# Finding the edges of 16 graphs on VectorE, and showing by sums that a matrix holds only zeros and ones

## The chip, the cores and the metric

The kernel runs on one core of a Trainium2 chip. The metric is the device time of one run in microseconds; lower is better. Five engines work side by side: TensorE (PE, with its weight loads as PEld), VectorE (DVE), ScalarE (ACT), GpSimd (POOL) and SyncE (SP, which here only issues transfers).

## The reference, cut to what matters

There are 16 graphs of 1024 nodes with 64 features each. `adj` is a symmetric float32 matrix of zeros and ones, drawn at random, 1024 x 1024 for each graph. Layer 0 thins the neighbours of each node, takes three weighted quantiles of their features and runs a small MLP; layer 1 is three graph convolutions.

```python
h = jnp.maximum(_layernorm(x), 0.0)
# layer 0
adj_ = jnp.where(eye, 1.0, adj);  neigh = (adj_ > 0) & ~eye
rank = jnp.cumsum(ni, axis=-1) - ni;  nb = ni.sum(-1)         # ni = neigh as int
skip = jnp.where(nb > 10, (nb + 1) // 2, 1)
rem = neigh & (skip > 1) & (rank % skip == skip - 1) & mask   # then rem | rem^T
nd = where(rem, 0, adj_) > 0                                  # the live neighbours
s = jnp.sort(where(nd[..., None], h[:, None], inf), axis=2)   # quantiles 0.25, 0.5, 0.75
x = x + (relu((h + agg) @ W1 + b1) @ W2 + b2) * mask
# layer 1
h = jnp.maximum(_layernorm(x), 0.0)
x1 = bn(relu(adj @ (h @ W1) + b1)); x2 = ...; x3 = ...        # adj as it is, not only its sign
x = x + relu(concat(x1, x2, x3) @ Wl + bl)
```

What matters for the change is that layer 0 only asks whether an entry is above zero, while layer 1 multiplies with the entries themselves. A kernel that stores the matrix as one byte of 0 or 1 per entry is right for both only if every entry is exactly 0 or 1. Both kernels therefore carry a flag that says whether any entry was something else; if it is raised, a second, general path computes everything again. With the inputs here the flag stays down.

## The kernel before

**Pairs.** The graphs go in eight pairs. `prepare(p, pools)` makes all that layer 0 needs of pair p; it is written as a generator, and each `yield` in it ends a step. The main part first runs `prepare(0)` to its end, with nothing beside it. Then, for each pair, it goes through seven blocks of nodes (`gather_block`, `sort_block`), and before each block it takes 11 steps of the next pair's `prepare`. So pairs 1 to 7 are prepared under the gathering and sorting of the pair before. After the last pair's preparation come its own blocks, woven with the second phase (`later`: the MLP and layer 1), and then the flag.

**Order.** A scheduler fixes the order of the instructions on each engine when the kernel is built; it follows the order of the program loosely, and an engine then takes its instructions strictly in that order. Buffers of one tag in a pool are used in rotation, in the order of the program: a tag with `bufs=1` has one buffer, so that the next user of the tag must wait until the one before it is done. Within a pool all calls share the tags, so graph x=0 and graph x=1 of a pair do.

**Preparing one graph** (`prepare_one`, L651 to L844). The matrix goes through in eight tiles of 128 rows:

- a transfer on SP's queue loads the tile `a`, 512 KB of float32, into one of two buffers (L661);
- ACT takes the sign of it into `edge`, one byte an entry (L662);
- DVE computes (a == 1) != a with one instruction, which is 1 where an entry is neither 0 nor 1, and sums it along each row into `odd` (L664); the entries themselves go to a scrap tile `junk_v`;
- PE transposes the tile of `edge` by eight matmuls with the identity into `ptE` in PSUM (L669), in one of two buffers of the tag "big";
- ACT copies `ptE` to `edgeT` (L672).

After the eight tiles `edgeT` is written to DRAM for layer 1 (L676), and the neighbours are counted and ranked: sums over chunks (L648), a few small DVE instructions, eight matmul groups with ACT (`stays`, L717) and DVE (L718), eight with ACT again (L744, which overwrites `edge` with the live neighbours and sums them into `nv`). The nodes are then ranked by the number of live neighbours: eight ACT passes (L762), each of which compares `keys` with one node per row and writes its entries to a scrap tile of the tag "junk" (one buffer), while the sums go to `above`. DVE turns those into `place` (L765), and POOL sends the rows of `edge` to their places in DRAM (L770).

When both graphs are that far, `find_live` reads the rows back and transposes them to `liveT` (L786 to L799), and checks by sums that the degrees lie where the blocks expect them: `by` compares sums with a table `bounds` (L817), and L820 sums what is beyond, with its entries going to the tag "junk" too. `number_slots` numbers the neighbours of each node into `r` (L838). `prepare` ends with `z` (L611 to L614) and the features in three bfloat16 parts, `hp` (L620 to L624).

**Gathering.** For each block and group of slots DVE compares `r` with the slot's number into `s` (L962, two buffers), PE multiplies `s` with `hp` into `pg` (L993), and ACT copies it to `g` (L998). `sort_block` sorts `g` on DVE (L920 and others).

**Bounds and flag.** The table `bounds` is made at setup, L470 to L490: POOL fills lines of 1024 and sends them to rows of `bounds` by transfers, 16 lines with two transfers each. The flag, L1409 to L1424, takes the largest of `odd` in each row and the largest of `beyond`, brings the rows together with one transpose on PE, and compares with 0.

Of the kernel before, what the change touches and what calls it, by code (L numbers as in the profile page):

```python
# [9 lines left out]
F32 = mybir.dt.float32  # L10
F16 = mybir.dt.float16
BF16 = mybir.dt.bfloat16
F8 = mybir.dt.float8e4
# [3 lines left out]
ALU = mybir.AluOpType  # L17
# [4 lines left out]
P = 128  # L22
# [377 lines left out]
def graph_layers_kernel(ctx: ExitStack, tc: tile.TileContext, ins, out: bass.AP):  # L400
# [61 lines left out]
    bounds = const.tile([C, HALF], BF16, name="bounds")  # L462
# [7 lines left out]
    with tc.tile_pool(name="setup", bufs=2) as setup:  # L470
        for c in range(1, NT + 1):
            most, least = [(-float(N), 0, N)], [(0.0, 0, N)]
            for (j0, j1, few, slots), (first, end, fewer) in zip(BLOCKS + (TAIL,), NEAR):
                if c == NT:
                    least.append((float(few), j0, j1))
                    most.append((-float(slots), j0, j1))
                    for k in sorted(fewer, reverse=True):
                        most.append((-float(k), j0, j0 + fewer[k]))
                if c in first:
                    most.append((-float(first[c]), j0, j1))  # L480
                if c in end:
                    least.append((float(end[c]), j0, j1))
            for row, pieces in ((c - 1, most), (NT + c - 1, least)):
                line = setup.tile([1, N], BF16, tag="line", name="line")
                for value, a, b in pieces:
                    nc.gpsimd.memset(line[:, a:b], value)
                for hf in range(NH):
                    nc.gpsimd.dma_start(
                        out=bounds[32 * hf + row : 32 * hf + row + 1, :], in_=line[:, hf * HALF : (hf + 1) * HALF]
                    )  # L490

    odd = const.tile([P, NB, NT], F32, name="odd")
# [74 lines left out]

    h_d = [dram.tile([N, C], F32, name=f"h_d{b}") for b in range(NB)]
# [14 lines left out]
    def prepare(p, pools):  # L583

        work, keep, ps = pools
        st = Pair()
        st.p = p
# [63 lines left out]
    def prepare_one(st, x, pools):  # L651
# [7 lines left out]
        for t in range(NT):  # L659
            a = work.tile([P, N], F32, tag="a", bufs=2, name="a")  # L660
            nc.sync.dma_start(out=a, in_=adj_d[b, t * P : (t + 1) * P, :])  # L661
            nc.scalar.activation(edge[:, t, :], a, AF.Sign, saturate=False)  # L662
            junk = work.tile([P, N], F8, tag="junk_v", name="junk_v")
            nc.vector.scalar_tensor_tensor(  # L664
                junk, a, 1.0, a, ALU.is_equal, ALU.not_equal, accum_out=odd[:, b, t : t + 1], saturate=False
            )
            pt = ps.tile([P, NT, P], F32, tag="big", bufs=2, name="ptE")
            for u in range(NT):
                nc.tensor.matmul(  # L669
                    out=pt[:, u, :], lhsT=edge[:, t, u * P : (u + 1) * P], rhs=ident_h, start=True, stop=True  # L670
                )
            nc.scalar.activation(edgeT[:, :, t * P : (t + 1) * P], pt, AF.Copy, saturate=False)  # L672
            if t % 2:
                yield
# [105 lines left out]
        def find_live():  # L780
# [31 lines left out]
            for hf in range(NH):  # L812
# [4 lines left out]
                    out=by[:, sl], lhsT=ident_h[rows, rows], rhs=bounds[rows, :], start=False, stop=True  # L817
# [531 lines left out]
    with ExitStack() as stack:  # L1349
# [7 lines left out]
        with ExitStack() as inner:  # L1357
# [3 lines left out]
            )  # L1361

# [46 lines left out]
    with ExitStack() as stack:  # L1409
        ps = stack.enter_context(tc.tile_pool(name="ps_flag", bufs=1, space=PSUM))  # L1410
        most_odd = const.tile([P, 1], F32, name="most_odd")
        nc.vector.tensor_reduce(most_odd, odd.rearrange("p b t -> p (b t)"), AX.X, ALU.max)
        worst = const.tile([P, 1], F32, name="worst")
        nc.vector.tensor_copy(worst, most_odd)
# [6 lines left out]
        nc.vector.tensor_reduce(most, pd, AX.X, ALU.max)  # L1421
        nc.vector.tensor_scalar(most, most, 0.0, None, ALU.is_gt)
# [30 lines left out]
```

## Time and profile before

| | us |
|---|---|
| three runs of the kernel | 3240.37, 3244.12, 3251.95 (median 3244.12) |
| the profiled execution | 3232.01 |
| its span in the profile | 3230.2 |
| DVE busy | 2569.1 (80%) |
| PE busy | 2602.9 (81%) |
| ACT busy | 1714.2 (53%) |
| POOL busy | 461.8 (14%) |
| L664, DVE check of a tile | 156.3 in 128 instructions of 1.221 |
| L669, PE transposes of a tile | 1024 matmuls |
| L762, ACT ranking passes | 144.4 in 128 instructions of 1.128 |
| L962, DVE compares for gathering | 621.1 in 1312 instructions |
| L993, PE gathering matmuls | 1361.8 in 16848 instructions |
| load of `a`, issue to landing | 3.4 |

The profile is of one execution, and its span is 1.8 us shorter than that execution's own time. An engine's share is its busy time over the span, an average over stretches that have different limits. The mean granted TensorE clock in this execution is 0.902 of the full one. In the tables of groups, the words after the line and the engine are the operation, what it writes <- what it reads, and the shapes; then come the busy time in us, the mean of one in ns, and the idle time of that engine just before these instructions with what ended most of it. In a timeline each row is a start in us from the span's start, a length, the engine, the line and the operation, and in square brackets a wait that ended just before with what ended it.

### The profile page before, as it was taken

How to read it: one execution, taken by the hardware profiler on the slowest of the kernel's cores; microseconds unless marked ns; L12 is line 12 of the kernel's file. 1: busy time of each engine (PE TensorE's matmuls, PEld its weight loads, DVE VectorE, ACT ScalarE, POOL GpSimd, SP SyncE). 2: the span in 40 equal slices, each digit the busy share in tenths (PEclk: the TensorE clock that was granted, in tenths of full speed). 3: DMA queues.
4: the chain of work that ended last, by engine and by line, in shares of the span. 5: the costliest groups of instructions: out<-in, count | busy, mean ns of one | idle time of the engine just before them, and what ended most of it. 6: DMA issues, size and time to landing. Idle time of an engine off the chain costs nothing. (4 is left out here: it accounts for less than half of the span.)

```text
span 3230.2 us, 67236 instructions
## 1 busy us (share of the span) xinstructions
PE 2602.9 (81%) x27819; PEld 1728.7 (54%) x27849; DVE 2569.1 (80%) x5895; ACT 1714.2 (53%) x3292; POOL 461.8 (14%) x545
## 2 busy tenths in 40 slices
PE   3689968987898689867686799689976689898878
PEld 2446645664566357545463466456644356565545
DVE  4149999899889988998997889988996888793332
ACT  4777647655766566666464666476553223242221
POOL 4111020110011001200112010201112120221110
PEclk9779989998999799988797799889988799899999
DMA  4131113011311130114001211130102110222211
GB/s 136 46 105 66 37 44 123 33 35 32 118 33 37 42 107 33 51 54 97 31 17 45 91 48 34 45 117 32 39 21 61 21 42 17 54 55 53 53 53 41
DMA packets 221082, 177.45 MB, mean 55 GB/s; under 512 B 189024, under 2 KB 189152, under 8 KB 216672
## 3 DMA queue, kind: packets, MB, share of 16 engines
q1 hardware_dynamic: 141824, 125.88, 12.7%
q0 software_dynamic: 17408, 37.81, 3.8%
q10 hardware_dynamic: 61536, 9.39, 1.9%
q8 instruction: 219, 3.59, 0.5%
q14 instruction: 95, 0.78, 0.1%
HBM read 124.44 MB, written 48.55 MB: 54 GB/s over the span
## 5 line engine op out<-in xcount | busy, mean ns | idle before, releaser
L993 PE MATMUL pg<-s,hp 128*64 128x400 bf16 (+11 forms) x16848 | 1361.8, 314 | 93.2 <-DVE s L962 92.7
L993 PEld LDWEIGHTS <-hp 128*64 128x64 bf16 x16848 | 907.4, 113 | 452.1 <-issue 75.3
L962 DVE TENSOR_SCALAR s<-r 128x3200 bf16<-128x3200 bf16 (+25 forms) x1312 | 621.1, 520 | 144.2 <-PE pg L993 143.9
L998 ACT COPY g<-pg 128x400 f32<-128x400 f32 (+10 forms) x384 | 168.5, 442 | 478.2 <-PE pg L993 440.4
L920 DVE TENSOR_TENSOR t<-g 128x600 f32<-128x600 f32 (+9 forms) x524 | 319.8, 628 | 12.9 <-ACT g L998 11.1
L770 POOL DMA_INDIRECT live_d<-edge,place x128 | 175.4, 1371 | 1025.3 <-DVE place L765 870.9
L1129 PE MATMUL pg<-adjT,xw 128*64 128x512 fp8e4 x2304 | 285.5, 400 | 39.6 <-DVE xw L1119 28.9
L920 DVE TENSOR_TENSOR g<-t 128x96 f32<-128x96 f32 (+16 forms) x555 | 285.8, 539 | 1.4
L855 ACT ACTIVATE coef<-z,bias 128x200 f32<-128x200 f32 (+6 forms) x480 | 174.8, 402 | 140.9 <-DVE agg L933 133.7
L1129 PEld LDWEIGHTS <-xw 128*64 128x64 bf16 x2304 | 144.7, 115 | 163.1 <-DVE xw L1119 30.3
L1172 POOL DMA_INDIRECT agg<-agg_d,place x128 | 139.4, 1089 | 535.7 <-PE pt L1060 412.8
L920 DVE TENSOR_TENSOR t<-t 128x192 f32<-128x192 f32 (+20 forms) x447 | 208.5, 478 | 0.4
L796 PE MATMUL pt<-ident_h,lp 128*128 128x128 bf16 x1024 | 102.3, 261 | 120.8 <-DMA lp<-live_d 71.1
L786 POOL DMA_DIRECT2D lp<-live_d x128 | 87.5, 685 | 774.0 <-PE pt L796 745.4
L664 DVE SCALAR_TENSOR_TENSOR junk_v<-a 128x1024 fp8e4<-128x1024 f32 x128 | 156.3, 1221 | 49.2 <-DMA a<-in_adj 49.0
L858 ACT ACTIVATE coef<-coef,wcol 128x200 f32<-128x200 f32 (+7 forms) x512 | 190.7, 399 | 3.5 <-issue 2.2
L799 ACT ACTIVATE liveT<-pt 128x1024 fp8e4<-128x1024 f32 x128 | 129.9, 1024 | 98.7 <-PE pt L796 97.6
L838 ACT CAST r<-pr 128x592 bf16<-128x592 f32 (+1 forms) x256 | 143.5, 587 | 48.6 <-PE pr L834 47.4
L832 PE MATMUL pr<-liveT,upto 128*128 128x512 fp8e4 (+2 forms) x384 | 124.7, 343 | 50.3 <-ACT r L838 41.3
L796 PEld LDWEIGHTS <-lp 128*128 128x128 fp8e4 x1024 | 82.9, 117 | 145.0 <-DMA lp<-live_d 101.0
L762 ACT ACTIVATE junk<-keys,minus 128x1024 fp8e4<-128x1024 f32 x128 | 144.4, 1128 | 29.8 <-PE keys L755 28.7
L744 ACT ACTIVATE edge<-q,bias 128x1024 fp8e4<-128x1024 f32 x128 | 142.0, 1110 | 33.1 <-PE q L739 29.1
(182 smaller groups left out, 3956.6 us busy)
## 6 DMA issues: line engine op xcount, KB each, us to landing
a<-in_adj SPq DMA_DIRECT2D x128, 512.0 KB, 3.4
adjT_d<-edgeT SPq DMA_DIRECT2D x16, 1024.0 KB, 4.4
lp<-live_d POOLq DMA_DIRECT2D x128, 128.0 KB, 2.3
adjT<-adjT_d SPq DMA_DIRECT2D x16, 1024.0 KB, 6.3
room<-in_x SPq DMA_DIRECT2D x16, 256.0 KB, 3.2
h_d<-room SPq DMA_DIRECT2D x16, 256.0 KB, 2.9
h_again<-h_d SPq DMA_DIRECT2D x16, 256.0 KB, 3.8
xt<-in_x SPq DMA_DIRECT2D x16, 256.0 KB, 4.7
```

The lines of the kernel that those rows point to most:

```text
L664: nc.vector.scalar_tensor_tensor(junk, a, 1.0, a, ALU.is_equal, ALU.not_equal, accum_out=odd[:, b, t : t + 1], saturate=False)
L762: nc.scalar.activation(junk, keys, AF.Sign, bias=minus[:, t : t + 1], accum_out=above[:, t : t + 1], saturate=False)
L770: sent = nc.gpsimd.indirect_dma_start(out=live_d[b][:, :], out_offset=bass.IndirectOffsetOnAxis(ap=place[:, b, t : t + 1], axis=0), in_=ed ...
L796: nc.tensor.matmul(out=pt[:, u, :], lhsT=lp[:, u * P : (u + 1) * P], rhs=ident_h, start=True, stop=True)
L838: nc.scalar.copy(st.r[side][:, x, u, :], pr[:, : j1 - j0])
L855: nc.scalar.activation(coef[:, i, :], z[:, at], AF.Abs, bias=bias(rank - (slots + 1) // 2 + tau), scale=sign)
L858: nc.scalar.activation(coef[:, i, :], coef[:, i, :], AF.Relu, bias=wcol[:, q : q + 1], scale=-w)
L920: nc.vector.tensor_tensor(view(bufs, o, n1, n2), view(bufs, a, n1, n2), view(bufs, b, n1, n2), ALU.max if op else ALU.min)
L962: nc.vector.tensor_scalar(s[:, k, :, us, w0:], r[:, :, us, at + w0 : at + W], float(LIVE + 1 + k0 + k), None, ALU.is_equal)
L993: nc.tensor.matmul(out=pg[x * C : (x + 1) * C, ks, w0:], lhsT=st.hp[:, part, x, u, :], rhs=s[:, ks, x, u, w0:], start=(whole and i == 0 an ...
L998: nc.scalar.copy(g[:, k0 : k0 + n, :], pg)
L1129: nc.tensor.matmul(out=pg[cs, :], lhsT=part[:, u, cs], rhs=adjT[x][:, u, sl], start=(u == 0 and k == 0), stop=(u == NT - 1 and k == len(xw ...
```

## The change

**Edges on DVE.** `edge` is now made by DVE: each entry is compared with 1, which gives 1 or 0. The instruction that made `odd`, and its scrap tile `junk_v`, are gone.

**Sums on ACT.** That the other entries are 0 is shown by three sums per row of each tile, all on ACT: `signs`, the sum of Sign over the tile; `negative`, the sum of Relu(-2^100 a), which is above 0 as soon as one entry is below 0; and `ones`, the sum of the entries that the copy to `edgeT` writes. If no entry is negative, and the number of positive entries equals the number of ones, every entry is 0 or 1. The first two are passes of their own over `a`, whose entries go to a scrap tile of the tag "junk", the one that ranking and L820 use; the third is a sum added to the copy that was there before.

**Flag.** It takes the sum of signs - ones over all tiles and rows, which needs a second transpose on PE, and the largest of `negative`.

**Bounds.** The table is no longer built at setup in its own pool. A function `make_bounds` builds it, with the same instructions, in the pool of `prepare` and just ahead of `prepare(0)`; its lines use the tag "sums" (two buffers), which the sums over chunks use too. `prepare` hands it on as `st.bounds`.

```diff
-    bounds = const.tile([C, HALF], BF16, name="bounds")
...
-    with tc.tile_pool(name="setup", bufs=2) as setup:
-        for c in range(1, NT + 1):
...
-    odd = const.tile([P, NB, NT], F32, name="odd")
+    signs, negative, ones = (const.tile([P, NB, NT], F32, name=k) for k in ("signs", "negative", "ones"))
...
+    def make_bounds(work):
+        bounds = work.tile([C, HALF], BF16, name="bounds")
+        for c in range(1, NT + 1):
...
+            for row, pieces in ((c - 1, most), (NT + c - 1, least)):
+                line = work.tile([1, N], BF16, tag="sums", bufs=2, name="line")
+                for value, a, b in pieces:
+                    nc.gpsimd.memset(line[:, a:b], value)
+                for hf in range(NH):
+                    nc.gpsimd.dma_start(
+                        out=bounds[32 * hf + row : 32 * hf + row + 1, :], in_=line[:, hf * HALF : (hf + 1) * HALF]
+                    )
+        return bounds
...
             nc.sync.dma_start(out=a, in_=adj_d[b, t * P : (t + 1) * P, :])
-            nc.scalar.activation(edge[:, t, :], a, AF.Sign, saturate=False)
-            junk = work.tile([P, N], F8, tag="junk_v", name="junk_v")
-            nc.vector.scalar_tensor_tensor(
-                junk, a, 1.0, a, ALU.is_equal, ALU.not_equal, accum_out=odd[:, b, t : t + 1], saturate=False
-            )
+            nc.vector.tensor_scalar(edge[:, t, :], a, 1.0, None, ALU.is_equal, saturate=False)
+
+            for scale, func, count in ((1.0, AF.Sign, signs), (-float(2**100), AF.Relu, negative)):
+                junk = work.tile([P, N], F8, tag="junk", name="junk")
+                nc.scalar.activation(
+                    junk, a, func, scale=scale, accum_out=count[:, b, t : t + 1], saturate=False
+                )
...
-            nc.scalar.activation(edgeT[:, :, t * P : (t + 1) * P], pt, AF.Copy, saturate=False)
+            nc.scalar.activation(
+                edgeT[:, :, t * P : (t + 1) * P], pt, AF.Copy, accum_out=ones[:, b, t : t + 1], saturate=False
+            )
...
-                    out=by[:, sl], lhsT=ident_h[rows, rows], rhs=bounds[rows, :], start=False, stop=True
+                    out=by[:, sl], lhsT=ident_h[rows, rows], rhs=st.bounds[rows, :], start=False, stop=True
...
+            early += (make_bounds(early[0]),)
...
-        most_odd = const.tile([P, 1], F32, name="most_odd")
-        nc.vector.tensor_reduce(most_odd, odd.rearrange("p b t -> p (b t)"), AX.X, ALU.max)
+        flat = "p b t -> p (b t)"
+
+        others = const.tile([P, 1], F32, name="others")
+        nc.vector.tensor_tensor(signs, signs, ones, ALU.subtract)
+        nc.vector.tensor_reduce(others, signs.rearrange(flat), AX.X, ALU.add)
         worst = const.tile([P, 1], F32, name="worst")
-        nc.vector.tensor_copy(worst, most_odd)
+        nc.vector.tensor_reduce(worst, negative.rearrange(flat), AX.X, ALU.max)
...
+        po = ps.tile([1, P], F32, name="po")
+        nc.tensor.transpose(po, others, ident)
+        sum_others = const.tile([1, 1], F32, name="sum_others")
+        nc.vector.tensor_reduce(sum_others, po, AX.X, ALU.add)
+        nc.vector.tensor_tensor(most, most, sum_others, ALU.max)
```

## The prediction

> **What bounds the kernel now.** I read the page's engine shares first, then busy time by stage, then timelines of the places where the changed instructions stand.
>
> ```profile
> span 3230.2 us, 67236 instructions
> PE 2602.9 (81%) x27819; PEld 1728.7 (54%) x27849; DVE 2569.1 (80%) x5895; ACT 1714.2 (53%) x3292; POOL 461.8 (14%) x545
> ...
> L664 DVE SCALAR_TENSOR_TENSOR junk_v<-a 128x1024 fp8e4<-128x1024 f32 x128 | 156.3, 1221 | 49.2 <-DMA a<-in_adj 49.0
> ```
> ```profile
> 0.00:205.00 205.00, 105.44 (x833) 67.05 (x836) 55.98 (x202) 126.35 (x167) 67.23 (x172) 0.82 0.29 90
> 205.00:2200.00 1995.00, 1653.16 (x18988) 1106.55 (x19012) 1804.64 (x3986) 1224.43 (x2344) 221.37 (x210) 0.91 0.19 58
> ```
> The columns of the second are the stretch, its length, then busy time of PE, PEld, DVE, ACT, POOL. The first 205 us prepare pair 0 with nothing beside it: DVE works 27% of it and ACT 62%, so ACT and the latencies between engines set its end. From 205 to 2200 us the other pairs are prepared under the gathering and sorting of the pair before: DVE works 90% of that, PE 83%, ACT 61%. After 2200 us nothing of the change runs but the flag. So a microsecond of ACT costs in the first stretch, and one of DVE may cost in the second.
>
> ```profile
> 32.73 1.99 ACT L662 ACTIVATE edge<-a 128x1024 fp8e4<-128x1024 f32 x2
> ...
> 34.90 1.97 ACT L672 ACTIVATE edgeT<-ptE 128x1024 fp8e4<-128x1024 f32 x2
> ...
> 52.15 1.02 ACT L672 ACTIVATE edgeT<-ptE 128x1024 fp8e4<-128x1024 f32 x1 [0.21 <-PE ptE L669]
> ```
> ```profile
> 92.05 1.11 ACT L762 ACTIVATE junk<-keys,minus 128x1024 fp8e4<-128x1024 f32 x1 [2.40 <-PE keys L755]
> ...
> 93.16 1.01 ACT L672 ACTIVATE edgeT<-ptE 128x1024 fp8e4<-128x1024 f32 x1
> ...
> 106.70 1.11 ACT L762 ACTIVATE junk<-keys,minus 128x1024 fp8e4<-128x1024 f32 x1
> ...
> 107.90 1.02 ACT L672 ACTIVATE edgeT<-ptE 128x1024 fp8e4<-128x1024 f32 x1
> ```
> These are ACT's timeline in the first stretch: graph 0's edges and copies from 32.73 to 53.2 us, and then graph 1's eight copies, woven into graph 0's eight ranking passes (L762) from 92.05 to 108.9, because graph 1's edges had been made before.
>
> ```profile
> 307.00 1.11 ACT L762 ACTIVATE junk<-keys,minus 128x1024 fp8e4<-128x1024 f32 x1
> ...
> 308.24 1.11 ACT L762 ACTIVATE junk<-keys,minus 128x1024 fp8e4<-128x1024 f32 x1
> ```
> Two passes into the one junk buffer start 1.24 us apart; with a copy between (92.05, 93.16) a pass holds ACT 1.11 us.
>
> ```profile
> L662 ACT ACTIVATE edge<-a x128: 1039/1057/1105, 32.7 to 2183.5; 128x1024 fp8e4<-128x1024 f32 x128
> ...
> DMA to landing us min/median/max: 3.0/3.4/5.6
> ```
> ```profile
> L611 DVE TENSOR_SCALAR half<-nvs x8: 693/694/694, 194.6 to 2416.2; 128x1024 f32<-128x1024 f32 x8
> ```
> ```profile
> 1225.00:1255.00 30.00, 29.80 (x384) 23.26 (x384) 21.52 (x26) 20.69 (x44) 10.88 (x10) 1.00 0.16 50
> ```
> A load of `a` lands 3.4 us after issue. The last line is the place just after graph 6's ranking, where PE is full and DVE waits for it.
>
> **What the Trainium skill says.** "VectorE: DVE Perf Modes", section "The perf-mode tier table (the rule you actually need)": an fp32 tensor_scalar from SBUF runs at twice the rate of an operation with two tensors. The trace agrees: L611 takes 0.694 us for 1024 elements, L664 1.221. The same page, "Two Vector instructions with no wait between them", says that an accumulator output makes a second instruction; the trace shows it (0.08 us behind each L664, 0.19 behind each L762). "ScalarE: Activation LUTs", section "What ACT_TABLE_LOAD costs": 186 ns plus 0.833 ns an element, and 93 ns of overlap between neighbours. That gives 1.04 us and a hold of 0.95; L662 takes 1.057 and the next starts 0.95 later.
>
> **The change, part by part.**
> DVE, per tile: L664 holds DVE 1.15 us (1.22 less 0.07 to 0.08 of overlap). Its successor has one fp32 source, so I take L611's 0.69, hold 0.61. No row has this form with an 8-bit output; the other bound is no gain at all, 1.22. Saving 0.54 x 128 = 69 us, of which 16 tiles (9 us) lie in the first stretch, where DVE idles.
>
> ACT, per tile: Sign 0.95 and copy 0.92 become Sign 1.11, Relu 1.11 and a summing copy of about 1.05 (0.92 and up to 0.19 for the read): 1.87 becomes 3.27, and 0.13 more wherever two junk passes are neighbours. That is 1.4 x 128 = 179 us more on ACT. Under 205-2200 us it has idle time for its 157 us share.
>
> Order. Edges are now DVE's, so PE's transposes hang on DVE's queue. More important, Sign and Relu take the buffer `junk` that ranking also takes, and buffers of a tag go round in the order of the program: graph x=1's Signs can't start before graph x=0's ranking. The order of the changed program's instructions shows it: in every pair graph 1 gets only two edges early (the two `a` buffers), and six stand behind `place`; before, all eight stood earlier. Two `a` buffers then tie each load to the Relu two tiles before.
>
> First stretch. Graph 0: 8 x 3.27 + 0.3 (ln_var) + ten neighbours x 0.13 = 27.8 us from 32.73, end 60.5 instead of 53.2: +7.3. Ranking thus starts at 99.4. It is now two passes alternating with two copies (4.1 us) and six neighbours (7.4): 110.9. Then graph 1's 16 passes and six copies, 16 x 1.11 + 6 x 1.05 + nine neighbours x 0.13 = 25.3; the last copy ends one pass earlier, at 135.1, where it ended at 108.9. Everything of graph 1, and so the first gather, comes **26 us later**; nothing else works then, so nothing hides it.
>
> 205-2200 us, per pair. (1) First graph's edges stand between the s comparisons (L962) of block 0. In the profile of before they take 1133 to 1158 and PE is busy with its gathers of 4 us each; DVE's saved 4 us go into waits for loads that hang on ACT. Followed tile by tile, with 3.4 us a load and ACT's order, the fourth comparison group comes about 1 us earlier: -1. (2) Between there and ranking DVE is 97% busy and loses eight L664 while gaining two compares, 8 us; PE is 91% busy in the same 50 us, so I let 3 us through: -3. (3) Behind `place`, six edges are fed by loads every 3.2 us or so (Sign, Relu and what ACT does between). Before, DVE waited for PE here:
> ```profile
> 931.36 1.59 DVE L962 TENSOR_SCALAR s<-r 128x2800 bf16<-128x2800 bf16 x2 [1.91 <-PE pg L993]
> ...
> 935.42 0.64 DVE L962 TENSOR_SCALAR s<-r 128x1824 bf16<-128x1824 bf16 x1 [2.47 <-PE pg L993]
> ```
> The last edge's data lands about 946 instead of s being written at 940: DVE is 5.6 us late, PE 3: +3. So -1 a pair, seven pairs, **-7**, with 5 us either way for each pair.
>
> Rest: `bounds` keeps its count of POOL memsets and transfers; they ended at 46 us and the first `sums` comes at 63: 0 while that cover of 17 us stands. The flag's extra transpose and reductions stand before the last pair's second layer in the order: under 1 us, taken as 1. Sum +26 - 7 + 1 = **+20**. On the profiled execution of 3232.0 us this is 3252; on the median of 3244.1, 3264.
>
> **Rivals.**
> A, DVE's gain comes through: DVE at 90% in 1995 us says so, PE's 83% and the loads against. All 60 us through gives +27 - 60 = -33, 3211; at 27 of the 60 it breaks even. It would need waits of s on PE (110.8 us in 200-2200) not to grow.
> B, the loads starve DVE: its order has eight edges within 11.5 us of work while ACT's order needs 32.6 us for them in a steady pair, and 15.7 against 6.8 behind `place`. If DVE stands the 16 and 9 us with no other cover, 7 x (25 - 9) = +112, 3382 with the start; half of it, +56, makes 3327. PE's own fullness there speaks against the whole.
> C, the compare runs at L664's rate: no saving on DVE, so (1) and (2) vanish and edges cost 3.6 us more behind `place`: +27 + 7 x 6 = +69, 3313. The table speaks against it.
> D, the start is covered: if graph 1's passes wove with something else it would cost 7; the order shows nothing else there.
>
> **How the numbers follow.** Forecast (start lost, pairs about even, +8 to +38) 0.62; A 0.14; B half or more 0.15; C 0.05; D or a mixture near zero 0.04. Time: 3264. Range 3236 to 3316: it leaves out most of A's gain and B's upper half. The forecast's own range is 3250 to 3284. Within 0.3% (about what a measurement here can tell, 10 us): D, the low edge of the forecast and the shallow part of A: 0.16. Faster 0.12, slower 0.72.
>
> **What would show it.** ACT's last graph-1 copy of pair 0 at about 135 us and the first s at about 231 rather than 205; a compare of 0.69; Sign and Relu near 1.06 with 0.19 reads; idle before edge on DVE of 60 to 120 us where L664 had 49; s waiting on PE about as before. A first s near 205 refutes the start; a pair's period (307 us before) shorter by over 4 us means A, longer by over 5 means B or C.

## The result and the profile after

The changed kernel takes 3295.31 us (median of 4 runs, 3279.17 to 3298.86), the kernel before 3244.40 (4 runs, 3240.37 to 3251.95). The ratio is 1.0145, 95% interval 1.0119 to 1.0171: 47 us slower. It lies inside the range that was given and on the forecast side, but the forecast was +20, so more than half of the loss was not foreseen.

The page of the changed kernel first (its profiled execution took 3298.52 us). A group's columns are the busy time and the mean in ns, then the idle time of the engine before it and what ended it.

```profile
span 3296.8 us, 67640 instructions
PE 2606.1 (79%) x27820; PEld 1714.4 (52%) x27850; DVE 2508.1 (76%) x5770; ACT 1867.7 (57%) x3804; POOL 451.7 (14%) x545
...
L669 ACT ACTIVATE junk<-a 128x1024 fp8e4<-128x1024 f32 x256 | 269.6, 1053 | 22.6 <-DMA a<-in_adj 18.5
...
L665 DVE TENSOR_SCALAR edge<-a 128x1024 fp8e4<-128x1024 f32 x128 | 88.8, 695 | 150.9 <-DMA a<-in_adj 141.9
```

The terms of work came out near the sums: a compare takes 0.695 us, DVE is busy 61 us less (69 in the prediction) and ACT 153 us more (179). What stands out is the idle time in the last line: DVE stood idle 150.9 us ahead of the edges, where it had stood 49.2 ahead of L664.

Busy time by stage, the same two stretches as in the prediction (stretch, length, then PE, PEld, DVE, ACT, POOL):

```profile
0.00:205.00 205.00, 86.46 (x731) 56.95 (x732) 42.45 (x180) 130.89 (x208) 64.23 (x165) 0.83 0.28 84
205.00:2200.00 1995.00, 1618.22 (x18478) 1069.91 (x18505) 1711.20 (x3813) 1316.95 (x2702) 217.27 (x218) 0.91 0.18 55
```

In the same 1995 us of the second, PE does 35 us less, DVE 93 less and ACT 93 more. Two things are mixed in this. DVE has less to do, and the stretch no longer holds the same work: in the changed kernel its first 27 us still belong to the preparation of pair 0. The table by pairs below keeps the two apart.

ACT's timeline in the first stretch, for the places shown of the kernel before:

```profile
97.56 1.11 ACT L769 ACTIVATE junk<-keys,minus 128x1024 fp8e4<-128x1024 f32 x1 [2.45 <-PE keys L762]
98.66 1.01 ACT L677 ACTIVATE edgeT<-ptE 128x1024 fp8e4<-128x1024 f32 x1
...
107.94 1.11 ACT L769 ACTIVATE junk<-keys,minus 128x1024 fp8e4<-128x1024 f32 x1
109.18 1.06 ACT L669 ACTIVATE junk<-a 128x1024 fp8e4<-128x1024 f32 x1
...
135.34 1.02 ACT L677 ACTIVATE edgeT<-ptE 128x1024 fp8e4<-128x1024 f32 x1 [0.61 <-PE ptE L674]
```

Two copies are woven into ranking, then the second graph's passes begin, and its last copy ends at 136.4 us where it ended at 108.9. The first `s` comes at 231.8 instead of 205.4.

**Where the rest went.** The trace gives a timetable of each pair: the first gathering matmul of the pair (every 2106th of the 16848 of L993, L1000 after) and the two `place` instructions. Summed over the seven pairs that are prepared under another ("the fifth pair" and the like count by the pair that is being gathered):

| us | first gather | gather to place 0 | place 0 to place 1 | place 1 to next gather | last pair's first gather to the end |
|---|---|---|---|---|---|
| before | 207.3 | 760.2 | 640.1 | 829.3 | 793.3 |
| after | 233.8 | 749.3 | 691.1 | 825.1 | 797.4 |
| difference | +26.5 | -10.9 | **+51.0** | -4.2 | +4.1 |

These add up to the 66.5 us between the two profiled spans; the medians of the runs are 51 us apart, so some 16 us of the 66.5 are the spread of single executions. The start is 26.5, as forecast. The pairs, forecast at -7, are +36, and all of it lies between the first graph's `place` and the second's. That step grew by 7.8 to 10.0 us in six of the seven pairs and shrank by 2.2 in the fifth. Here is DVE's timeline of this step in the fourth pair, first before and then after (a bracket is a wait and what ended it):

```profile
1235.17 0.17 DVE L765 TENSOR_SCALAR place<-above 128x8 int32<-128x8 f32 x1
...
1249.35 3.03 DVE L962 TENSOR_SCALAR s<-r 128x2112 bf16<-128x2112 bf16 x4 [2.75 <-PE pg L993]
...
1325.16 0.17 DVE L765 TENSOR_SCALAR place<-above 128x8 int32<-128x8 f32 x1
```
```profile
1292.59 0.17 DVE L772 TENSOR_SCALAR place<-above 128x8 int32<-128x8 f32 x1
...
1298.75 0.69 DVE L665 TENSOR_SCALAR edge<-a 128x1024 fp8e4<-128x1024 f32 x1 [1.43 <-DMA a<-in_adj]
1301.87 0.71 DVE L665 TENSOR_SCALAR edge<-a 128x1024 fp8e4<-128x1024 f32 x1 [2.43 <-DMA a<-in_adj]
...
1305.30 0.69 DVE L665 TENSOR_SCALAR edge<-a 128x1024 fp8e4<-128x1024 f32 x1 [1.22 <-DMA a<-in_adj]
...
1309.05 0.69 DVE L665 TENSOR_SCALAR edge<-a 128x1024 fp8e4<-128x1024 f32 x1 [2.51 <-DMA a<-in_adj]
1311.37 0.69 DVE L665 TENSOR_SCALAR edge<-a 128x1024 fp8e4<-128x1024 f32 x1 [1.63 <-DMA a<-in_adj]
...
1315.80 0.69 DVE L665 TENSOR_SCALAR edge<-a 128x1024 fp8e4<-128x1024 f32 x1 [1.79 <-DMA a<-in_adj]
1316.41 0.79 DVE L969 TENSOR_SCALAR s<-r 128x2464 bf16<-128x2464 bf16 x1
...
1390.44 0.16 DVE L772 TENSOR_SCALAR place<-above 128x8 int32<-128x8 f32 x1
```

DVE waits 11.0 us for six loads and writes the last `s` of the block 24.6 us after `place`; in the same pair before, that `s` was written at 17.2.

DVE's lateness is not what the second `place` hangs on, though. That is the second graph's last copy to `edgeT`, on ACT, here before and after:

```profile
1256.12 3.11 ACT L672 ACTIVATE edgeT<-ptE 128x1024 fp8e4<-128x1024 f32 x3 [0.69 <-PE ptE L669]
```
```profile
1324.59 1.01 ACT L677 ACTIVATE edgeT<-ptE 128x1024 fp8e4<-128x1024 f32 x1
```

It ends 24.1 us after the first `place` before and 33.0 after. In six pairs (all but the fifth) it ends at 23 to 25 us before and at 33 to 36 after, and in both kernels the second `place` follows 65 to 68 us behind it. What makes these copies late is ACT's queue. From the first `place` on, ACT works through the second graph's passes almost without a gap (23.8 of 24.8 us). The small copy `o` that ends the block stands behind most of them, at 22.3 us after `place` instead of 15.9, and PE waits 4.44 us for it, with transposes of the second graph behind it in PE's queue. Before, then after:

```profile
1251.11 0.27 ACT L1007 COPY o<-pt_agg 128x128 f32<-128x128 f32 x1
```
```profile
1314.92 0.26 ACT L1014 COPY o<-pt_agg 128x128 f32<-128x128 f32 x1
...
1315.24 0.33 PE L1012 MATMUL pt_agg<-ident,agg 128*128 128x128 f32 x1 [4.44 <-ACT o L1014]
```

The run junk_edge, below, has these copies nearly as late while DVE writes its `s` on time.

The waits of DVE from 205 to 2200 us, of the kernel before and then of the changed one (total, times, longest):

```profile
DVE s L962 <- PE pg L993: 110.8, 53, 21.3
DVE junk_v L664 <- DMA a<-in_adj: 33.8, 38, 2.8
DVE t L920 <- ACT g L998: 10.0, 11, 1.1
DVE half L611 <- ACT nvs L809: 9.8, 6, 1.8
```
```profile
DVE s L969 <- PE pg L1000: 130.0, 64, 11.4
DVE edge L665 <- DMA a<-in_adj: 82.8, 48, 3.4
DVE half L614 <- ACT nvs L816: 36.9, 7, 30.1
DVE t L927 <- ACT g L1005: 22.8, 21, 2.2
```

DVE waits 49 us longer for `a`, 13 longer for ACT's copies of `g` and 19 longer for PE. The line of `half` is no loss in the pairs: 30.1 us of it is the end of pair 0's preparation, which before lay ahead of 205 us. PE's own waits for `s` did not grow (51.6 us before, 49.7 after), but its wait for ACT's `o` is new, and the kernel before has none (same stretch):

```profile
PE pt_agg L1012 <- ACT o L1014: 23.7, 5, 5.7
```

### The profile page after: what moved, and what is told of

Its sections match the earlier page's. It is cut to its first block, busy times and chain, and to the rows that moved or that the text cites. A ratio compares the mean times of both kernels' runs of the same rounds, so it can differ in the third digit from the quotient of the medians.

```text
span 3296.8 us, 67640 instructions
## 1 busy us (share of the span) xinstructions
PE 2606.1 (79%) x27820; PEld 1714.4 (52%) x27850; DVE 2508.1 (76%) x5770; ACT 1867.7 (57%) x3804; POOL 451.7 (14%) x545
## 5 line engine op out<-in xcount | busy, mean ns | idle before, releaser
L1000 PE MATMUL pg<-s,hp 128*64 128x400 bf16 (+11 forms) x16848 | 1375.2, 315 | 84.6 <-DVE s L969 60.7
L1000 PEld LDWEIGHTS <-hp 128*64 128x64 bf16 x16848 | 897.3, 113 | 465.9 <-issue 93.2
L669 ACT ACTIVATE junk<-a 128x1024 fp8e4<-128x1024 f32 x256 | 269.6, 1053 | 22.6 <-DMA a<-in_adj 18.5
L665 DVE TENSOR_SCALAR edge<-a 128x1024 fp8e4<-128x1024 f32 x128 | 88.8, 695 | 150.9 <-DMA a<-in_adj 141.9
L674 PE MATMUL ptE<-ident_h,edge 128*128 128x128 bf16 x1024 | 95.7, 250 | 99.2 <-DVE edge L665 80.2
L845 ACT CAST r<-pr 128x592 bf16<-128x592 f32 (+1 forms) x256 | 141.9, 588 | 40.4 <-PE pr L841 39.2
```

The source lines that it names most:

```text
L669: nc.scalar.activation(junk, a, func, scale=scale, accum_out=count[:, b, t : t + 1], saturate=False)
L845: nc.scalar.copy(st.r[side][:, x, u, :], pr[:, : j1 - j0])
L1000: nc.tensor.matmul(out=pg[x * C : (x + 1) * C, ks, w0:], lhsT=st.hp[:, part, x, u, :], rhs=s[:, ks, x, u, w0:], start=(whole and i == 0 an ...
```

## The experiments

Every kernel is compared with runs of the kernel before on the same chip; the ratios are therefore what is compared. "us" is the ratio's distance from 1 times 3242 us, and carries about 4 to 12 us of uncertainty; a difference between two rows carries up to about 16.

| kernel | ratio | 95% interval | us |
|---|---|---|---|
| changed kernel | 1.0145 | 1.0119 to 1.0171 | +47 |
| own_junk | 1.0257 | 1.0221 to 1.0294 | +83 |
| no_relu | 0.9981 | 0.9967 to 0.9994 | -6 |
| no_sums | 0.9794 | 0.9759 to 0.9829 | -67 |
| no_check | 0.9790 | 0.9755 to 0.9825 | -68 |
| scrap_edgeT | 1.0001 | 0.9981 to 1.0021 | 0 |
| read_edge | 0.9935 | 0.9916 to 0.9955 | -21 |
| junk_edge | 1.0026 | 1.0014 to 1.0038 | +8 |
| relu_added | 0.9962 | 0.9947 to 0.9976 | -12 |
| relu_edge | 0.9888 | 0.9855 to 0.9922 | -36 |
| stt_edge | 0.9875 | 0.9845 to 0.9906 | -41 |
| before_lp | 1.0191 | 1.0163 to 1.0218 | +62 |
| bounds_only | 1.0002 | 0.9990 to 1.0013 | +1 |
| abs_sum | 0.9995 | 0.9975 to 1.0015 | -2 |
| mixed | 0.9981 | 0.9970 to 0.9993 | -6 |
| three_a | 0.9984 | 0.9969 to 0.9999 | -5 |
| two_a | 0.9973 | 0.9956 to 0.9990 | -9 |

The timetable as above, in the profiled executions, for those that the argument rests on:

| us | first gather | gather to place 0 | place 0 to place 1 | place 1 to next gather |
|---|---|---|---|---|
| before | 207.3 | 760.2 | 640.1 | 829.3 |
| after | 233.8 | 749.3 | 691.1 | 825.1 |
| junk_edge | 213.4 | 738.6 | 675.4 | 813.8 |
| scrap_edgeT | 216.7 | 770.6 | 637.7 | 812.4 |
| read_edge | 216.9 | 748.5 | 638.3 | 808.6 |
| no_sums | 198.1 | 722.1 | 643.4 | 809.3 |
| no_check | 206.3 | 702.7 | 645.7 | 816.1 |
| stt_edge | 206.9 | 720.8 | 649.3 | 818.4 |
| relu_added | 212.4 | 762.9 | 638.6 | 808.7 |
| relu_edge | 210.6 | 736.0 | 641.9 | 810.4 |

**A stall that only the old order has.** One pair must be set apart before any row is compared with the kernel before. The fifth pair takes 379 to 382 us in the four kernels that keep the old order (before, bounds_only, two_a, three_a), and 355 to 368 in all the other fourteen. In those four, one of POOL's moves of rows takes 14.4 us there, where those behind it take 1.0 to 1.5. PE then waits for the live rows, with the gathers behind them in its queue, and DVE waits 21.3 us for PE. From the kernel before:

```profile
1689.02 14.40 POOL L770 DMA_INDIRECT live_d<-edge,place  x1 [0.30 <-issue]
```
```profile
1714.41 1.89 PE L796 MATMUL pt<-ident_h,lp 128*128 128x128 bf16 x16 [22.35 <-DMA lp<-live_d]
```

PE's longest wait for live rows in that pair is 2 to 13 us in the others. Why that one move takes so long is not shown. Even abs_sum, which leaves the loads and DVE's work as they were, is 21 us shorter in that pair, so this gain came with every new order tried here. Every row but those of bounds_only, two_a and three_a thus has 14 to 27 us of it in its distance from the kernel before, the changed kernel 17.5. Differences among those rows are hardly touched.

### The order undone: own_junk, which failed, and why

```diff
 # changed kernel, ranking
-            junk = work.tile([P, N], F8, tag="junk", name="junk")
+            junk = work.tile([P, N // 4], I32, tag="lp", bufs=2, name="junk_r").bitcast(F8)
```

> The changed kernel, but ranking (the passes over keys) writes its scrap to a buffer of the tag lp, so that Sign and Relu share junk only with the pass over by. Nothing of the work changes: the same 256 passes, the same two buffers of a. In the order of DVE all eight edges of the second graph now stand ahead of the first graph's place. Theory 1 (the loss is the order that the shared scrap buffer forces): the first s comes at about 212 to 216 us instead of 231.8 (only graph 0's 7 us and a little more are lost), a pair's period falls from about 317 to 308, the idle time of DVE before edges behind place is gone; time about 3244 + 8 + 0 = 3252, at most 3262. Rival (the loss is the sheer work of ACT, 179 us more, and the loads held by Relu, wherever they stand): first s above 225, periods of 314 and more, time 3280 or more.

It came out at +83 where theory 1 had about +10, and the first gather, at 234.2 us, was no earlier than in the changed kernel. Yet the order in the pairs was undone: the second `place` stood at 190 to 193 us of a pair in five of the seven, where the changed kernel has it at 198 to 201. The time was lost behind it: the first graph's live rows, read into `lp`, now waited for the second graph's ranking. The kernel before with that one edit shows it.

> The kernel before with one edit, ranking's scrap written to the tag lp, as own_junk has it. Theory (own_junk lost its gain to this: the loads of the first graph's live rows must wait for the second graph's ranking): first s about 20 us later, periods about 11 us longer, liveT only after the second place; 3242 + 20 + 7 x 10 = about 3330, at least 3310. Rival (own_junk was slow for another reason): 3240 to 3255.

It costs 62 us, a little less than expected. The waits of `lp` there (us, times until):

```profile
L786 POOL DMA_DIRECT2D lp<-live_d x112: 536/537/2566, 412.8 to 2438.5; - x112
its engine sat idle before it (us, times) until:
  ACT junk_r L762: 542.8, 14
```

Fourteen times in seven pairs, once for each of the two buffers, a load of live rows waits for ranking; in the kernel before the same list has no such wait, and the first of these loads went out at 325.1 us instead of 412.8. So own_junk had replaced one wait by another and decides nothing about the first. Some 20 us of its loss stay unexplained by before_lp, 14 of them ahead of the first gather (234.2 us against 220.0).

### The order undone without a new wait: scrap_edgeT

```diff
 # changed kernel, Sign and Relu
-                junk = work.tile([P, N], F8, tag="junk", name="junk")
                 nc.scalar.activation(
-                    junk, a, func, scale=scale, accum_out=count[:, b, t : t + 1], saturate=False
+                    edgeT[:, :, t * P : (t + 1) * P], a.rearrange("p (u j) -> p u j", u=NT), func,
+                    scale=scale, accum_out=count[:, b, t : t + 1], saturate=False,
                 )
```

> The changed kernel, but Sign and Relu write their scrap to the piece of edgeT that the copy of the same tile overwrites later, and not to junk; ranking keeps junk. own_junk had moved ranking's scrap to the tag lp, whose two buffers the loads of live rows need too: its liveT starts 13 us later after the second place than the kernel before has it (192 to 226 after a place at 191, against 181 to 215 after 193), and in the first stretch 20 us later. Theory 1 (the order forced by the shared scrap costs, and own_junk hid it behind that new wait): the second place stays at 191 to 192 us of a pair, liveT starts at 180 again, the first s comes at about 214, periods are 306 to 309; time 3295 - 20 - 7 x 8 = about 3220. Rival (it is ACT's work itself that delays everything behind it, and lp had no part): liveT starts at 190 or later, periods 315 and more, time 3290 or more.

All 47 us are gone; the time is that of the kernel before. The timetable shows where: place 0 to place 1 falls from 691.1 to 637.7, the first gather from 233.8 to 216.7. The gain is 47 of the 75 that theory 1 expected, since gather to place 0 grew from 749.3 to 770.6, where more of the second graph's edges now stand (they begin 30 us into the pair and end at 80, ahead of ranking at 90). So the shared scrap buffer is worth the whole net loss, but it isn't the only cost. The passes themselves kept their length (a median of 1.056 us in both), and PE's wait for the copy `o` is gone.

### The passes and the loads they hold: no_relu, no_sums, read_edge, junk_edge

no_relu drops Relu from the loop, no_sums drops Sign too (then `signs` is set to `ones`, and `negative` to 0). read_edge and junk_edge have one edit each:

```diff
 # read_edge, against scrap_edgeT
-                    edgeT[:, :, t * P : (t + 1) * P], a.rearrange("p (u j) -> p u j", u=NT), func,
+                    edgeT[:, :, t * P : (t + 1) * P], edge[:, t, :].rearrange("p (u j) -> p u j", u=NT), func,
 # junk_edge, against the changed kernel
-                    junk, a, func, scale=scale, accum_out=count[:, b, t : t + 1], saturate=False
+                    junk, edge[:, t, :], func, scale=scale, accum_out=count[:, b, t : t + 1], saturate=False
```

> The changed kernel without the Relu pass: that no entry is negative is left out, the order and the shared scrap buffer stay. ACT loses 128 passes of 1.06 us, and a load waits only for Sign. Theory 1 (order): second graph's six edges still stand behind place; with one pass a tile instead of two they come every 2.5 us or so instead of every 3.4, so about half of the loss goes: first s about 218 (231.8 less 8 x 1.1 less some of graph 0's), periods about 312, time about 3265. Rival (ACT's work): about the same here in the first stretch, but periods back at 308 and less because the removed 128 passes are the larger part of what was added; time 3245 to 3250.

> The changed kernel with neither Sign nor Relu: edges made by DVE's compare, the sum on the copy stays, the signs and negatives are left out. It prices edges on DVE alone. Theory 1: nothing ties the edges to ranking any more, they go ahead of place again; a load is let go by DVE. First s about 205 to 209; periods 302 to 305 (the 8 us of DVE relief that lies ahead of the first place is worth 3 to 4); time about 3215 to 3230. Rival (edges on DVE's queue are themselves the loss, since PE's transposes now stand behind the sorting): periods of 310 or more, time above 3255.

> As scrap_edgeT, but Sign and Relu read the tile of edge instead of a, so that entries other than 1 go untested; the number and size of ACT's passes stay. A load of a is then let go by DVE's compare alone. Theory 2 (loads held by ACT's passes cost too): idle time of DVE before edges falls to 35 us as in no_sums, and the time falls by 10 to 30 us below scrap_edgeT. Rival (ACT's time in its own queue costs, not the loads): the same time as scrap_edgeT within 8 us.

> The changed kernel with Sign and Relu still writing to junk, as ranking does, but reading the tile of edge instead of a (entries other than 1 go untested). Against the changed kernel only the loads are set free of the ordered passes; against read_edge only the scrap buffer is shared again. Theory (the shared buffer costs its 53 us through the loads: a buffer of a can't be let go before passes that must follow ranking, so six edges stand behind place): within 12 us of read_edge, 3215 to 3230. Rival (the passes that stand behind ranking delay the second graph's copies by themselves): 3255 or more.

no_sums is 67 us faster than the kernel before: edges on DVE are no loss but a gain. It is more than twice what theory 1 gave, but 23 us of it lie in the fifth pair, where the stall is gone. no_relu, at 3235.7 us, lies below both expectations. From no_sums the loss can be built up one property at a time: 256 passes on ACT that hold no load, +46 (read_edge); that they hold the loads, +21 (scrap_edgeT; the idle time of DVE before edges, 53.7 and 63.5 us, moves less than expected); that they share ranking's scrap, +47 (the changed kernel). With the -67 this makes the +47. The passes over `edge`, one byte an entry, take 1.05 us as those over `a` do, so these runs change what is held and not how much work there is.

junk_edge, +8, lies between its two theories. Sharing the buffer costs 30 us even where no load hangs on it: passes behind ranking delay the second graph's copies by themselves. The last of these copies ends 32 us after the first `place` (24 to 26 us in read_edge, 33 to 36 in the changed kernel; the fifth pair apart), place 0 to place 1 is 675.4 against 638.3, and PE's wait for the copy `o` is there (21.8 us), while DVE's edges wait for loads no longer than L664 did before (35.8 us against 33.8), and the last `s` of the block shown above is written 17.4 us after `place`, as it was before. With the loads tied to it the same sharing costs 47.

### What the removed DVE instruction had cost: no_check, stt_edge, relu_added, relu_edge

```diff
 # kernel before, L664
 # no_check: the instruction left out;  stt_edge:
-                junk, a, 1.0, a, ALU.is_equal, ALU.not_equal, accum_out=odd[:, b, t : t + 1], saturate=False
+                junk, edge[:, t, :], 1.0, edge[:, t, :], ALU.is_equal, ALU.not_equal, accum_out=odd[:, b, t : t + 1], saturate=False
 # relu_added (relu_edge reads edge[:, t, :] instead of a):
+            nc.scalar.activation(
+                junk, a, AF.Relu, scale=-float(2**100), accum_out=odd[:, b, t : t + 1], saturate=False
+            )
```

> The kernel before without the 128 scalar_tensor_tensor of L664: the test of the entries is left out, edges stay on ACT. DVE loses 147 us (128 x 1.15), 18 of them in the first stretch, where it idles. It prices what relief of DVE is worth. Theory (3 of 8 us come through ahead of place, nothing where DVE waits for PE): 4 to 5 us a pair, time about 3244 - 30 = 3214, first s unchanged at 205. Rival A of the prediction (DVE at 90% is the bound, relief comes through whole): 3244 - 125 = 3120. The other end (PE bounds it, relief is worth nothing): 3240 or more.

> The kernel before, with L664 reading the tile of edge instead of a (entries other than 1 go untested): the same 128 instructions with two sources on DVE, but a load of a is let go by ACT's sign alone. no_check took 65 us of 147 us of DVE work away and freed the loads at once; this tells them apart. Theory (the relief was the load that waited for its turn in DVE's queue): most of the 65 us come without any relief of DVE, 3242 - 45 = about 3197 (as a ratio 0.986 or less). Rival (DVE's time is the bound): 3242, as a ratio 0.997 or more.

> The kernel before, in which the scalar_tensor_tensor of L664 is replaced by the Relu pass on ACT with a scrap buffer of its own (the test for values between 0 and 1 and above 1 is left out). So edges stay on ACT, well ahead, and nothing is ordered by ranking; against no_check it adds 128 passes of ACT, 143 us with their accumulator reads. Theory 1 (order, not work): at most 15 us above no_check, 3180 to 3195. Rival (ACT's work counts wherever it stands, as Relu's 59 us between no_relu and the changed kernel suggest): 3225 to 3240.

> As relu_added (the kernel before with a Relu pass on ACT in place of L664), but Relu reads the tile of edge instead of a, so it doesn't hold a load. relu_added came 56 us above no_check. Theory (a pass of ACT costs by its time in ACT's queue, about 0.2 us of each 1.1, and the rest by the load it holds): 20 to 25 us above no_check, a ratio of 0.985 to 0.988. Rival (all of it is ACT's own time): as relu_added, 0.994 to 0.998.

no_check gains 68 of DVE's 147 us, twice the theory. stt_edge keeps all of DVE's work and still gains 41, a little less than its theory. Its instructions took as long as before (1.220 us), so this part of what L664 cost was not DVE's time: it was the buffer of `a` that L664 held until its turn came in DVE's queue. By the ratios it is three fifths (41 of 68 us, each by 10 either way or so). Both gains contain the stall of the fifth pair; in the profiles of the six other pairs it is 20 of 38 us, about half. SP's timeline shows the loads, with ten loads around the start of the fifth pair in the kernel before, in no_check and in stt_edge (start, time from the first issue to the last):

```profile
1424.25 36.86 SPq L661 DMA_DIRECT2D a<-in_adj  x10
```
```profile
1403.67 26.57 SPq L662 DMA_DIRECT2D a<-in_adj  x10
```
```profile
1414.31 26.24 SPq L661 DMA_DIRECT2D a<-in_adj  x10
```

The ten loads take 37 us where DVE must have read them, and 26 to 27 where it need not. With them the first graph's copies end 36 to 38 us after the pair's first gather in the kernel before, and 31 to 32 in the other two (the first of the seven pairs apart). The last two kernels price a pass of ACT in the place where the kernel before has its own: against no_check, 128 passes cost 56 us, 32 of them as ACT's time (relu_edge) and 24 through the held load (relu_added). Theory 1 of relu_added, that ACT's work costs nothing outside a bad order, is refuted.

### Small parts: bounds_only and abs_sum

bounds_only makes the table of bounds as the change does, in the kernel before.

> The kernel before with only the table of bounds moved, as the change moves it. Theory: nothing, since it is ready before the first sums: 3236 to 3248, first s at 205. Rival (its lines take the buffers of sums, and POOL's part comes later): the first s later by 5 us or more.

No difference, as expected (first gather 207.7 us). abs_sum replaces L664 by the compare alone, summed, and has the copy to `edgeT` sum absolute values:

```diff
-            nc.vector.scalar_tensor_tensor(
-                junk, a, 1.0, a, ALU.is_equal, ALU.not_equal, accum_out=odd[:, b, t : t + 1], saturate=False
+                nc.vector.tensor_scalar(
+                    junk, a, 1.0, 0.0, ALU.is_equal, ALU.add, accum_out=ones[:, b, t : t + 1], saturate=False
                 )
-            nc.scalar.activation(edgeT[:, :, t * P : (t + 1) * P], pt, AF.Copy, saturate=False)
+                nc.scalar.activation(
+                    edgeT[:, :, t * P : (t + 1) * P], pt, AF.Abs, accum_out=nonzero[:, b, t : t + 1], saturate=False
+                )
```

> The kernel before with another test of the entries that leaves nothing out: edges stay ACT's signs, the copy to edgeT takes the absolute value and sums it (nonzero entries), and DVE's compare with 1 only sums (ones); all entries are 0 or 1 if the sums agree. DVE's instruction has one source now. If it runs at 0.69 us as the changed kernel's compare does: 0.53 x 128 = 68 us less on DVE, of which no_check's 65 of 147 says 30 come through, and the summing copy adds 0.1 x 128 = 13 us on ACT, at most 6 of it through: about 3218. If the sum as an output holds it at 1.2: no gain, 3240 to 3255.

It gained nothing by DVE, and its group says why:

```profile
L665 DVE TENSOR_SCALAR_CACHE_REDUCE junk_v<-a 128x1024 fp8e4<-128x1024 f32 x128 | 155.5, 1215 | 48.5 <-DMA a<-in_adj 48.1
```

The compare with a sum as a second output is another instruction and takes 1.215 us, not 0.695. The Trainium skill has this in "SBUF — State Buffer", section "Who interferes with whom": of tensor_scalar, the form that also writes out its accumulator is left out of the operations that can enter the two-port modes. The two groups agree with it. DVE is thus left as it was. What the sums on the copies to `edgeT` cost isn't shown by this run: its -2 us contain the 21 us of the fifth pair, so they may cost up to about that much.

### Attempts at a better kernel: mixed, three_a, two_a

mixed has even tiles as in scrap_edgeT and odd tiles as before. three_a is the kernel before with a third buffer for `a`, room for it being made by four edits that two_a has alone.

> Nothing is left out: even tiles as in scrap_edgeT (edge by DVE's compare, Sign and Relu on ACT, summed copy), odd tiles as in the kernel before (edge by ACT's sign, scalar_tensor_tensor on DVE), scrap in edgeT's own piece for both. If each way costs more the more tiles it has (each engine's queue has some room): 3200 to 3230, below both. If each tile costs its half microsecond either way (65 us for 128 on DVE, 67 for 128 on ACT): 3235 to 3250.

> The kernel before with a third buffer for a, and nothing left out. Room for it: L664 writes its scrap back into a, ranking's scrap goes to edgeT of the same graph (no longer needed by then), the pass over by writes to by itself, and nvs (whole numbers) is kept in bfloat16. Theory (stt_edge: 40 of the 65 us are the load that waits for DVE's turn): a third buffer lets one more load run ahead, half of the 40 us or more comes through: ratio 0.988 to 0.994. Rival (three tiles stand behind DVE as two did): 0.997 to 1.002.

> The same edits as three_a with two buffers for a, so that the buffer alone is told apart. Both theories: as before, a ratio of 0.997 to 1.003; what three_a has below this is the buffer's.

mixed is 0.2% below the kernel before, as its second theory had it (about 3236 us), two_a 0.3%, three_a 0.2%: none by more than the bound set in the prediction, and the third buffer gives nothing. SP's timeline of three_a, the same ten loads:

```profile
1429.59 36.20 SPq L661 DMA_DIRECT2D a<-in_adj  x10
```

They still take 36 us. In the pair that starts at 1445.5 us in that profile, its third sign runs at -5.2 us of the pair and the fourth only at 6.8, after the first turn of DVE's check (L663 there) at 2.2: three tiles stand behind DVE as two did. Here a held load was a matter of when the last reader's turn comes, and not of one buffer more.

## Why the prediction was right and wrong

**Right.** The start: +26 forecast, +26.5 measured, with the steps on the way (graph 1's last copy at 135 us, measured 136.4; first s at about 231, measured 231.8). That the order follows from the shared scrap buffer, and what it does to the start, is shown by scrap_edgeT, which takes 17 of the 26 back. The compare (0.69 assumed, 0.695 measured) and the passes (1.056 and 0.19 for the read) had the right sizes, the move of the bounds cost nothing (bounds_only), and rival C fell with the compare. Step (2), DVE's relief ahead of ranking, was put at -3 a pair: from the first graph's last copy to place 0 the pairs are 3.7 us shorter on average.

**Wrong: step (3), the edges behind place.** It was put at +3 a pair; place 0 to place 1 grew by 51.0 us in seven pairs, and by 8.9 in each of six on average. The order was right (six edges, fed by loads that come slowly), and the delay of the edges was nearly so: the loads came every 3.4 us instead of 3.2, and the last edge was made 23.9 us after place where the step had about 21. What it had wrong is the path. It took the price to be DVE's lateness with `s`, "DVE is 5.6 us late, PE 3", with PE's work as a cover for the rest. The second `place` hangs on the second graph's own copies, which ACT's queue made 9 us later, and nothing covers that: place 1 follows the last copy by 65 to 68 us in both kernels. junk_edge shows that most of it needs no late `s` and no load held by ACT: 35 of the 51 us are there without them.

**Wrong: step (1), the first graph's edges.** It was put at -1 a pair. The first graph's last copy came 2.1 us later on average (39.2 us after the first gather, before 37.1), which is 15 us in seven pairs and turns a forecast of -28 for (1) and (2) into the -10.9 of gather to place 0. Two terms were both taken too small. Without the passes that copy ends at 33.6 us (no_sums), so edges on DVE are a gain of 3.5; it is no gain by earlier loads, since the ten loads around the start of the fifth pair take nearly as long there as the 36.86 us before:

```profile
1394.73 35.40 SPq L664 DMA_DIRECT2D a<-in_adj  x10
```

With passes that hold no load the copy ends at 36.9 (read_edge), with passes that hold them at 38.8 (scrap_edgeT). The step took the loss as a matter of waits for loads alone, and ACT's 157 us were let go with "it has idle time for its 157 us share". Most of it did go into idle time, but not all: no_sums to read_edge is 26 us in gather to place 0. ACT was idle 39% of that stretch; that what is left comes from the chain of edge, transposes and copy, which runs through ACT's queue, fits these times but no run takes it apart further.

**The rivals.** A's relief of 60 us is near the 67 of no_sums by luck. Its mechanism, DVE's time coming through whole, fails: between stt_edge and no_check, 147 us of DVE's time are worth 28. B is half confirmed. The prediction had named a period longer by over 5 us as the sign of B or C, and six of the seven periods grew by 5.6 to 16.3 us. Its half-way size was 3327, and the time fell between it and the forecast. But its mechanism, DVE standing for loads, is the smaller part behind `place` (junk_edge), and DVE's idle time before edges from 205 to 2200 us rose by 49 us, less than a third of B's 7 x 25 = 175. The idle time before edges in the whole run, 150.9 us, lies above the 60 to 120 that were given. D fell: nothing covered the start.

Three slips of the prediction change nothing here. The ranking at 1225 us is that of graph 8, counted from 0, and not of graph 6. B's 16 us do not follow from the 32.6 and 11.5 beside them, which differ by 21. And the second instruction behind a sum is stated of VectorE by the page that it names; on ACT the trace alone shows it (0.19 us behind each L762).

So the sign came out of a small sum of large terms: -67 for edges on DVE without L664 (some 20 of it the stall of the old order), +46 for the passes, +21 for the loads that they hold, +47 for the shared scrap buffer. The forecast had the shared buffer right in the start. In the pairs it sized it too small, and the other terms too, and it had no term for the stall.

## What to carry to other kernels

An instruction that reads a rotating buffer costs its own time and also the time that the buffer waits for its turn in that engine's queue: here the second was about half to three fifths of the whole, and a third buffer did not help. When an instruction is moved to an engine with idle time, ask where in the chain its new neighbours stand. With ACT idle 39% on average, most of the added passes was hidden, but what was not hidden (32 of about 142 us for 128 passes, 46 of about 284 for 256, at 1.11 us each) was as large as the whole net loss. A scrap tile shared by a tag is an order between its users, so give scrap a place that its own next step overwrites anyway, and look at what a new place ties together before believing that an order has been undone. To find what a late step hangs on, look in both traces for the event that it follows at a fixed distance. And compare stretch by stretch: a stall that happens to sit in the kernel before, as in the fifth pair here, looks like a gain of whatever edit moves it.

## What was not expected of the hardware

On DVE a tensor_scalar of 128x1024 float32 took 0.695 us, and with a sum as second output 1.215, as long as L664 with its two sources. ACT's ranking passes, where nothing stands between them, start 1.24 us or more apart into one scrap buffer (a median of 1.25 before), and 1.09 to 1.11 apart into two, here in before_lp:

```profile
1262.32 1.11 ACT L762 ACTIVATE junk_r<-keys,minus 128x1024 fp8e4<-128x1024 f32 x1 [1.21 <-PE keys L755]
1263.43 1.10 ACT L762 ACTIVATE junk_r<-keys,minus 128x1024 fp8e4<-128x1024 f32 x1
1264.52 1.11 ACT L762 ACTIVATE junk_r<-keys,minus 128x1024 fp8e4<-128x1024 f32 x1
```
